# Layer 1 of the first image moves to the other instruction stream, with part of the next image's layer 0 beside it

## The chip, the core and the metric

The kernel is one program on one core of a Trainium2 chip. The time is that of the device in microseconds (us), from launch to end. A profiled execution also has a span, from the first to the last instruction. PE is TensorE, DVE is VectorE, ACT is ScalarE, POOL is GpSimd, SP is SyncE (which only issues transfers).

## What is computed

Four images of 48 channels and 256 x 256 pixels pass through four residual layers, each on a group-normalised input (16 groups of 3 channels):

```python
x = x + L0(gn(x), ...)   # 1x1 conv to 288 channels, 3x3 depthwise; q, k, v of 96 channels;
                         # product of the spectra of q and k in 8x8 patches; layer norm; times v; 1x1 conv to 48
x = x + L1(gn(x), ...)   # 1x1 conv to 288; spectrum of each 8x8 patch times a mask; 3x3 depthwise;
                         # gelu(first half) * second half; 1x1 conv to 48
x = x + L2(gn(x), ...)   # running sums of the image; two 3x3 convs give a box per pixel; the sums at the
                         # box's four corners, gathered with bilinear weights, over the box's area
x = x + L3(gn(x), ...)   # 1x1 conv to 192, 3x3 depthwise, gelu gate, 1x1 conv to 48, spectrum times a mask
```

All of it is float32. The layers of one image follow each other, and each needs the statistics (mean and deviation of each group) of the whole image before it. Images don't depend on each other.

## The kernel before, in words

`run` (L1609 on) writes two streams of work, `a` and `b`, as Python generators. Stream a has the statistics of image 0, then layer 0 and layer 1 of images 0, 1, 2, 3 in turn, then layer 3 of the four images. Stream b has the preparation of layer 1's weights (`patch_weights`), of layer 3's (`taps`), the statistics of the other images, and then layer 2 of images 0, 1, 2, 3. A generator yields numbers, its planned cost in units of its own; the stream whose sum is smaller is advanced next. A layer starts only when the one before it on the same image is written, and the stream's sum is then raised to that one's. So layer 2 of image i is written between the pieces of layers 0 and 1 of image i + 1, that of image 3 between those of layer 3, and layer 1 of image 0 has nothing beside it.

The framework then orders the instructions of each engine by dependencies, with the order of writing as the priority; instructions given to `pinned` keep the order of writing among themselves on their engine. Every engine executes its own list in order. Tiles come from pools; stream a's lie on the left of SBUF and stream b's on the right.

- `bank` (L228) gives the next of PSUM's eight banks. Five belong to stream a and two to stream b; the eighth has the tag `w4` and holds layer 2's bilinear weights. When stream b is out of work (`alone`), a takes all eight in turn.
- `dma` (L237) issues stream a's transfers from SP and stream b's from POOL. Layer 1 issues most of its own from SP by name (`queue`, L745).
- `layer0`: 128 units, in software pipelining over eight steps. In a step, `convolve` (16 products of 288 columns by `convolve2`, L391, into four banks, which ACT copies to `qkv`, L483) and `inverse` come first, then a yield of 7, then `spectra`, `turn`, `project`, `gate`, and a yield of 7 again. Each two units need a strip of the image, six transfers into two tiles A and B (`columns2`, L293), in two buffers.
- `layer1` has three phases with HBM buffers between them. Phase A (L680 to L728): 16 strips of 16 blocks; each block and half is one product (L713) into a bank, which ACT or DVE copies to `hs` (L718 and L720), and a strip is stored to `hD`. It yields 3 for each two blocks. Phase B: 36 groups of 8 channels; `around` (L765) makes the rims of the patches by four small products (L771) and eight transfers `yh<-yb`; `gated` (L784), four times for each group, fills two banks by L788 and L794, then ACT makes the Gelu (L799) and DVE the product (L800). It yields 4 after each `gated` and each `around`. Phase C: 16 strips, four pieces of each; `turn` (L856 on) transposes three banks (L865), `project` (L871 on) adds two products into one (L877). It yields 5 for each piece.
- `layer2` first makes running sums (`sums`), then 33 x 4 steps of gathers by POOL (L1126, 16 of them each), the weighing on DVE and the two convolutions of later pieces on PE.

Of the kernel before, what the change touches and what calls it, by code (L numbers as in the profile page):

```python
# [8 lines left out]
F32 = mybir.dt.float32  # L9
# [183 lines left out]
class Net:  # L193
    def __init__(self, ctx, tc, a, out):
        self.tc, self.nc, self.a, self.out = tc, tc.nc, a, out
        self.nimage = a["x"].shape[0] // C

        self.banks = {
            f: ctx.enter_context(tc.tile_pool(name="ps" + f, bufs=n, space=PSUM)) for f, n in (("a", 5), ("b", 2))
        }  # L200
        self.stream, self.alone, self.turns = "a", False, 0
        self.const = ctx.enter_context(tc.tile_pool(name="const", bufs=1))
        self.dram = ctx.enter_context(tc.tile_pool(name="dram", bufs=1, space=DRAM))
        self.stat = ctx.enter_context(tc.tile_pool(name="stat", bufs=2))
        self.n, self.fused = 0, {}
        nc, a = self.nc, self.a
        self.ident = self.load("c_ident", [128, 128])
        dft = self.load("c_dft", [128, 5, 128])
        self.fq, self.fk, self.back, self.rf, self.ri = (dft[:, i, :] for i in range(5))
        self.sel = self.load("c_sel2", [48, 506])  # L210
        self.tapsel = self.load("c_tapsel2", [128, 4, 74])
        group = self.load("c_group", [112, 208])
        self.group = {CP: group[:CP, 112:208], 112: group[:, 0:112]}
# [13 lines left out]

    def bank(self):  # L228
        if self.alone:
            self.turns += 1  # L230
            if self.turns % 8 == 0:
                return self.banks["b"].tile([128, 512], F32, name=self.nm("ps"), tag="w4", bufs=1)
            if self.turns % 8 > 5:
                return self.banks["b"].tile([128, 512], F32, name=self.nm("ps"), tag="ps")
        return self.banks[self.stream].tile([128, 512], F32, name=self.nm("ps"), tag="ps")

    def dma(self, out, of):  # L237
        (self.nc.sync if self.stream == "a" else self.nc.gpsimd).dma_start(out, of)  # L238

    def pinned(self, instruction):  # L240

        return self.tc.keep_in_program_order(instruction)

    def pool(self, name, bufs):
# [146 lines left out]
    def convolve2(self, AB, W, n, j, to):  # L391

        nc = self.nc
        A, B = AB
        half = B.shape[1]

        def full(q, b):
            for g in range(3):
                nc.tensor.matmul(  # L399
                    to(q, b), A[:, j + half * q, 128 * b + g : 128 * b + g + 128], W[:, g, :],  # L400
                    start=b == 0 and g == 0, stop=b == 1 and g == 2,
                )

        def tails(b):
            for q in range(2):
                p = slice(64 * q, 64 * q + 58)
                nc.tensor.matmul(
                    to(q, b), B[p, j, 128 * b : 128 * b + 128], W[p, 3, :], start=b == 1, stop=b == 0
                )
# [32 lines left out]
    def layer0(self, x, mr, y, xb):  # L442
        nc, a = self.nc, self.a
        st = self.stat.tile([112, 129, 6], F32, name=self.nm("st"), tag="st" + self.stream, bufs=1)
        with ExitStack() as ctx:
# [39 lines left out]
            def spectra(t):  # L485
                t.t = []
                for f, c in ((self.fq, 0), (self.fk, 96)):
                    banks = [self.bank() for _ in range(2)]
                    for h in range(2):
                        p = slice(64 * h, 64 * h + 64)  # L490
                        nc.tensor.matmul(v3(banks[h]), f[p], t.qkv[p, :, c : c + 96], start=True, stop=True)  # L491
                    for h in range(2):
# [6 lines left out]
            def inverse(t):  # L499
# [5 lines left out]
                for h in range(2):  # L505
                    nc.tensor.matmul(po[64 * h : 64 * h + 64, 0:384], self.back[:, 0:64], t.t[h][:], start=True, stop=True)
                nc.scalar.copy(  # L507
# [33 lines left out]
            def turn(t):  # L541
                pt = self.bank()
                for b in range(4):
                    nc.tensor.transpose(pt[:96, 128 * b : 128 * b + 128], t.un[:, b, :], self.ident[:])
                t.u = sb.tile([96, 512], F32, name="u", tag=f"u{t.i}{t.j}", bufs=1)
                nc.scalar.copy(t.u[:], pt[:96, :])

            def project(t, other):
# [5 lines left out]
                for i, of in ((0, other), (1, t)):  # L554
                    n = 48 if i else 64
                    nc.tensor.matmul(pp[64 * i : 64 * i + n, :], pr[:, 0:n], of.u[:], start=True, stop=True)
                for q in range(2):
# [118 lines left out]
    def layer1(self, x, mr, y):  # L676
# [4 lines left out]
        with ExitStack() as ctx:  # L681
# [25 lines left out]
            for s in range(NS):  # L707
                xt = xts[s % 3]
                hs = sb.tile([128, 8 * NG, 2, 16], F32, name="hs", tag="hs")
                for b in range(16):  # L710
                    for h in range(2):
                        ps = self.bank()
                        nc.tensor.matmul(  # L713
                            ps[:, :288], xt[64 * h : 64 * h + 49, 128 * b : 128 * b + 128],
                            win[64 * h : 64 * h + 49], start=True, stop=True,
                        )
                        if h and b % 2:
                            nc.vector.tensor_copy(hs[:, :, h, b], ps[:, :288])  # L718
                        else:
                            nc.scalar.copy(hs[:, :, h, b], ps[:, :288])  # L720
                    if b == 7 and s + 2 < NS:
                        load(s + 2)
                    if b % 2:
                        yield 3
                of = hs[:].rearrange("p (g c) h b -> p g (c h b)", c=8)
# [3 lines left out]
        with ExitStack() as ctx:  # L729
# [35 lines left out]
            def around(t):  # L765

                for e in range(4):
                    ps = self.bank()
                    for i in range(2):
                        c = 4 * i + e  # L770
                        nc.tensor.matmul(  # L771
                            ps[64 * i : 64 * i + 64, :].rearrange("p (s n) -> p s n", n=32),
                            t.wr[:, 64 * c : 64 * c + 64], t.hg[:, :, c, :], start=True, stop=True,
                        )
                    if e % 2:
# [8 lines left out]
            def gated(t, e):  # L784
                both = [self.bank() for _ in range(2)]
                for i in range(2):
                    c = 4 * i + e
                    nc.tensor.matmul(  # L788
                        both[i][:].rearrange("p (s n) -> p s n", n=32), t.wd[:, 128 * c : 128 * c + 128],
                        t.hg[:, :, c, :], start=True, stop=False,  # L790
                    )
                for i in range(2):
                    p = slice(64 * i, 64 * i + 64)
                    nc.tensor.matmul(  # L794
                        order(both[i][:]), t.wd[p, 1024 + 128 * e : 1152 + 128 * e], pick(t.yh, e)[p],
                        start=False, stop=True,
                    )
                gl = sb.tile([128, 512], F32, name="gl", tag="gl")
# [15 lines left out]
            for g in range(NG):  # L814
                t = groups[g]
                for e in range(4):
                    gated(t, e)
                    yield 4
                    if e == 0 and g + 1 < NG:
                        around(groups[g + 1])  # L820
                        if g + 2 < NG:
                            rims(g + 2)
                        yield 4
                queue(gD[:, :, g, :], t.hg[:, :, 0:4, :].rearrange("p s c n -> p s (c n)"))
# [5 lines left out]
        with ExitStack() as ctx:  # L830
# [25 lines left out]
            def turn(s, j):  # L856
                gs, got = strips[s], []
                for q in range(3):
                    pt = self.bank()
                    for b in range(4):  # L860
                        if q < 2:
                            of = gs[:, 0:96, q, 4 * j + b]
                        else:
                            of = gs[:, 96:144, :, 4 * j + b].rearrange("p c h -> p (c h)")
                        nc.tensor.transpose(pt[:96, 128 * b : 128 * b + 128], of, self.ident[:])  # L865
                    gc = sb.tile([96, 512], F32, name="gc", tag=f"gc{q}")
# [4 lines left out]
            def project(s, j, got):  # L871
                xt, yt = buffers[s % 2]
                pp = self.bank()
                for last in range(2):
                    for h in range(2):
                        n = 48 if h else 64
                        nc.tensor.matmul(  # L877
                            pp[64 * h : 64 * h + n, :], pr[:, h if last else 2, 0:n], got[2 if last else h][:],
                            start=not last, stop=bool(last),
                        )  # L880
                whole = lambda t: t.rearrange("p (b r c) -> p b r c", b=4, r=8)
# [17 lines left out]
            for s in range(NS):  # L899
                for j in range(4):  # L900
# [6 lines left out]
                    if j == 3 and s + 2 < NS:  # L907
                        gated(s + 2)
                    yield 5
            project(*last)  # L910
# [698 lines left out]
    def run(self, layers=(0, 1, 2, 3)):  # L1609
# [4 lines left out]

        a = [("first", 0)] + [(n, i) for i in images for n in (0, 1) if n in layers] + [(3, i) for i in images if 3 in layers]
        b = ([("weights", 0)] if 1 in layers else []) + ([("taps", 0)] if 3 in layers else [])
        b += [("first", i) for i in images[1:]]
        b += [(2, i) for i in images if 2 in layers]
# [8 lines left out]
        def advance(f):  # L1627
            self.stream = f
            self.alone = not todo["b"]
            if now[f] is None:  # L1630
                n, i = todo[f][0]
                if n not in ("first", "weights", "taps"):
# [3 lines left out]
                    at[f] = max([at[f]] + [done[k] for k in need])  # L1636
                now[f] = self.first_statistics(i) if n == "first" else self.patch_weights() if n == "weights" else self.taps() if n == "taps" else self.layer(n, i)
            try:
                at[f] += next(now[f])
            except StopIteration:  # L1640
# [72 lines left out]
```

## Time and profile before

| | |
|---|---|
| median of 14 runs | 18,127.32 us (18,107.94 to 18,156.39) |
| the profiled execution | 18,110.35 us |
| its span | 18,108.4 us |
| mean granted PE clock | 0.927 |
| PE, weight loads, DVE, ACT, POOL busy | 90%, 54%, 63%, 34%, 50% |
| HBM | 2,377 MB read, 832 MB written |

Where the stages lie in that span, by the first and last matmul of their lines:

| stage | us from the span's start |
|---|---|
| layer 0 of image 0 (L399), with the preparations at first | 182 to 1,832 |
| layer 1 of image 0: A (L713), B (L788), C (L865) | 1,876 to 2,126; 2,167 to 2,798; 2,817 to 3,029 |
| layer 0 of image 1, beside layer 2 of image 0 | 3,082 to 4,951 |
| layer 1 of image 1, beside the same | 5,017 to 6,589 |
| the same of image 2, beside layer 2 of image 1 | 6,638 to 10,135 |
| the same of image 3, beside layer 2 of image 2 | 10,188 to 13,685 |
| layer 3 (L1439), beside layer 2 of image 3 until 17,235 | 13,745 to 18,075 |

In the lines of the profile, `L399 PE MATMUL ps<-W,A` is an instruction of line 399 that reads the tiles W and A and writes a PSUM tile. A float32 product is two instructions there. The view by stretches gives the busy time of each engine in a piece of the span, with the number of instructions, the granted clock of PE as a share of full speed, the busy share of the 16 DMA engines and the rate. The view of waits gives how long an engine stood before instructions of a line and what ended it: in total, how often, the longest.

### The profile page before, as it was taken

Reading aid. Unit: us, or ns where it says so; the run is one execution under the profiler, and the core shown is the slowest. Engines: PE = TensorE matmul, PEld = TensorE weight load, DVE = VectorE, ACT = ScalarE, POOL = GpSimd, SP = SyncE. Lnnn points to the kernel's source line nnn. Section 1 sums busy time; section 2 is a strip of 40 time slices with the busy share of each in tenths; the row PEclk is TensorE's granted clock in tenths of the full one; section 3 lists DMA queues with packets and bytes.
Section 4 is the critical chain, followed back from the end, with each engine's and each line's share of the span. In section 5 each row is a group of like instructions: output and inputs, shape, how many; then the busy total and the mean of one; then the engine's idle time right before and its main releaser. Section 6 shows DMA issues by size and latency. Waiting matters only on the chain. (4 is left out here: it accounts for less than half of the span.)

```text
span 18108.4 us, 223197 instructions
## 1 busy us (share of the span) xinstructions
PE 16376.4 (90%) x75610; PEld 9769.5 (54%) x75610; DVE 11484.8 (63%) x24628; ACT 6121.1 (34%) x12781; POOL 9007.0 (50%) x8933
## 2 busy tenths in 40 slices
PE   8999798999978889998888899988888998889899
PEld 3556424555543355555433555554336676767778
DVE  4554323577765555777656467776565788888866
ACT  2444523444441134444412344444122221212222
POOL 1200000377765534777666157776660577777700
PEclk9999899999979999999799999987988998989999
DMA  6642887555599975555999555559997888888867
GB/s 167 187 100 57 278 287 233 137 140 144 133 297 298 285 215 134 140 142 137 325 300 288 175 141 142 142 165 317 301 286 195 203 199 198 205 195 205 204 157 164
DMA packets 1770067, 3629.80 MB, mean 200 GB/s; under 512 B 505646, under 2 KB 1279883, under 8 KB 1631784
## 3 DMA queue, kind: packets, MB, share of 16 engines
q1 hardware_dynamic: 1236272, 2319.89, 44.1%
q0 software_dynamic: 448688, 1098.99, 23.2%
q10 hardware_dynamic: 83968, 196.64, 4.4%
q8 instruction: 603, 9.88, 0.2%
q14 instruction: 536, 4.39, 0.1%
HBM read 2377.26 MB, written 832.39 MB: 177 GB/s over the span
## 5 line engine op out<-in xcount | busy, mean ns | idle before, releaser
L1126 POOL DMA_INDIRECT V<-t,idx x8192 | 8575.5, 1047 | 3624.1 <-issue 2277.4
L399 PE MATMUL ps<-W,A 128*128 128x288 f32 x12288 | 3294.8, 417 | 38.0 <-ACT t L497 16.5
L399 PEld LDWEIGHTS ps<-W,A 128*128 128x128 f32 x12288 | 2281.0, 192 | 991.5 <-issue 306.8
L1138 DVE TENSOR_TENSOR V<-V,w 128x1536 f32<-128x1536 f32 x1024 | 1764.3, 1744 | 158.3 <-DMA V<-t,idx 124.5
L1146 DVE TENSOR_TENSOR V<-V 128x1536 f32<-128x1536 f32 (+3 forms) x2048 | 1817.5, 887 | 11.2
L483 ACT COPY qkv<-ps 128x288 f32<-128x288 f32 x2048 | 766.6, 399 | 2498.6 <-PE ps L399 1277.9
L238 POOL DMA_DIRECT2D X<-x x96 | 72.6, 757 | 2930.5 <-DMA x<-yt 2008.6
L1020 PE MATMUL ps<-A,W 128*96 128x512 f32 x3072 | 1476.6, 618 | 0.0
L511 DVE BATCH_NORM_STATS2 bs<-o 128x6 f32<-128x96 f32 x2048 | 381.1, 246 | 1394.3 <-ACT o L507 1393.9
L800 DVE TENSOR_TENSOR hg<-gl,ps 128x512 f32<-128x512 f32 x576 | 394.2, 685 | 1322.0 <-ACT gl L799 1305.5
L788 PE MATMUL ps<-hg,wd 128*128 128x512 f32 x2304 | 1143.2, 619 | 43.7 <-DMA wd<-wD 43.7
L713 PE MATMUL ps<-win,xt 49*128 49x288 f32 x4096 | 941.1, 562 | 154.1 <-ACT hs L720 99.2
L799 ACT ACTIVATE gl<-ps 128x512 f32<-128x512 f32 x576 | 343.8, 597 | 1991.4 <-PE ps L794 1946.8
L794 PE MATMUL ps<-yh,wd 64*128 64x512 f32 x2304 | 715.8, 695 | 312.6 <-DMA yh<-yb 232.7
L1474 ACT ACTIVATE y<-y 128x384 f32<-128x384 f32 x512 | 267.7, 523 | 2111.7 <-DVE y L1473 2087.5
L720 ACT COPY hs<-ps 128x288 f32<-128x288 f32 x1536 | 825.5, 685 | 407.6 <-PE ps L713 253.8
L1439 PE MATMUL ps<-W,A 128*128 128x192 f32 x4096 | 927.9, 350 | 18.9 <-DVE y L1463 14.1
L1020 PEld LDWEIGHTS ps<-A,W 128*96 128x96 f32 x3072 | 477.3, 167 | 864.1 <-issue 852.4
L1439 PE MATMUL ps<-wh,A 128*128 128x192 f32 x4096 | 830.7, 349 | 118.1 <-DVE y L1463 61.4
L491 PE MATMUL ps<-qkv,c_dft_sb 64*128 64x384 f32 x4096 | 884.6, 514 | 0.0
L713 PEld LDWEIGHTS ps<-win,xt 49*128 49x128 f32 x4096 | 636.2, 251 | 443.6 <-ACT hs L720 226.1
L1439 PEld LDWEIGHTS ps<-wh,A 128*128 128x128 f32 x4096 | 732.1, 205 | 213.2 <-issue 134.7
(211 smaller groups left out, 25487.4 us busy)
## 6 DMA issues: line engine op xcount, KB each, us to landing
hg<-hD SPq DMA_DIRECT2D x144, 2048.0 KB
hD<-hs SPq DMA_DIRECT2D x60, 4608.0 KB
A<-P SPq DMA_DIRECT2D x256, 773.2 KB
gD<-hg SPq DMA_DIRECT2D x144, 1024.0 KB
gs<-gD SPq DMA_DIRECT2D x64, 2304.0 KB
V<-t,idx POOLq DMA_INDIRECT x8192
xt<-b SPq DMA_DIRECT2D x128, 896.0 KB
wd<-wD SPq DMA_DIRECT2D x144, 768.0 KB
```

The source lines that it names most:

```text
L399: nc.tensor.matmul(to(q, b), A[:, j + half * q, 128 * b + g : 128 * b + g + 128], W[:, g, :], start=b == 0 and g == 0, stop=b == 1 and g == 2,
L483: nc.scalar.copy(t.qkv[:, 2 * q + b, :], banks[2 * b + q][:, 0:288])
L491: nc.tensor.matmul(v3(banks[h]), f[p], t.qkv[p, :, c : c + 96], start=True, stop=True)
L713: nc.tensor.matmul(ps[:, :288], xt[64 * h : 64 * h + 49, 128 * b : 128 * b + 128], win[64 * h : 64 * h + 49], start=True, stop=True,)
L720: nc.scalar.copy(hs[:, :, h, b], ps[:, :288])
L788: nc.tensor.matmul(both[i][:].rearrange("p (s n) -> p s n", n=32), t.wd[:, 128 * c : 128 * c + 128], t.hg[:, :, c, :], start=True, stop=False,
L794: nc.tensor.matmul(order(both[i][:]), t.wd[p, 1024 + 128 * e : 1152 + 128 * e], pick(t.yh, e)[p], start=False, stop=True,)
L1020: m = nc.tensor.matmul(to[q], W[:, g, :], A[:, 2 * q : 2 * q + 2, g : g + 256], start=q == 0 and g == 0, stop=q == 1 and g == 2,)
L1126: nc.gpsimd.indirect_dma_start(out=V[:, k, 4 * cr : 4 * cr + 4, :].rearrange("p e c -> p (e c)"), out_offset=None, in_=table, in_offset=ba ...
L1138: self.pinned(nc.vector.tensor_mul(Vm, Vm, wm.unsqueeze(2).to_broadcast([128, 32, 48])))
L1146: self.pinned(nc.vector.tensor_add(V[:, :, 0:n, :], V[:, :, 0:n, :], V[:, :, n : 2 * n, :]))
L1439: pin(nc.tensor.matmul(of(j, b), A[:, j, k, 128 * b : 128 * b + 128], four[j], start=start, stop=stop))
```

## The change

Layer 1 of image 0 (called `early`) leaves stream a and comes to stream b, between the statistics and layer 2 of image 0. Stream a goes on from layer 0 of image 0 to layer 0 of image 1. While `early` is being written, `crossed` is set, and then:

- the yields of layer 1 are multiplied by 0.18, 0.35 and 0.05 in its three phases (`light`), so that stream b is advanced more often;
- the matmuls and transposes of layers 0 and 1 that go through `pe` keep the order of writing on PE, both streams together;
- `dma` swaps its queues: stream b's transfers go to SP, stream a's to POOL;
- stream b's third bank is the one with the tag `w4`, every third time;
- in phase A DVE copies every second bank, where it was one in four.

Outside that stage, the yields of layer 2 are multiplied by 0.96 (`pace`).

```diff
+        if self.crossed and self.stream == "b":
+            self.turns += 1
+            if self.turns % 3 == 0:
+                return self.banks["b"].tile([128, 512], F32, name=self.nm("ps"), tag="w4", bufs=1)
         if self.alone:
...
     def dma(self, out, of):
-        (self.nc.sync if self.stream == "a" else self.nc.gpsimd).dma_start(out, of)
+        (self.nc.sync if (self.stream == "a") != self.crossed else self.nc.gpsimd).dma_start(out, of)
...
+    def light(self, n, share):
+        return n * share if self.crossed else n
+
+    def pe(self, instruction):
+        return self.pinned(instruction) if self.crossed else instruction
...
-                        if h and b % 2:
+                        if h and (b % 2 or self.crossed):
                             nc.vector.tensor_copy(hs[:, :, h, b], ps[:, :288])
                         else:
                             nc.scalar.copy(hs[:, :, h, b], ps[:, :288])
...
-                        yield 3
+                        yield self.light(3, 0.18)
...
                     gated(t, e)
-                    yield 4
+                    yield self.light(4, 0.35)
                     if e == 0 and g + 1 < NG:
                         around(groups[g + 1])
                         if g + 2 < NG:
                             rims(g + 2)
-                        yield 4
+                        yield self.light(4, 0.35)
...
-                    yield 5
+                    yield self.light(5, 0.05)
...
-        a = [("first", 0)] + [(n, i) for i in images for n in (0, 1) if n in layers] + [(3, i) for i in images if 3 in layers]
+        early = (1, 0) if 1 in layers and len(images) > 1 else None
+        a = [("first", 0)] + [(n, i) for i in images for n in (0, 1) if n in layers and (n, i) != early]
+        a += [(3, i) for i in images if 3 in layers]
+        pace = {(2, i): 0.96 for i in images}
         b = ([("weights", 0)] if 1 in layers else []) + ([("taps", 0)] if 3 in layers else [])
-        b += [("first", i) for i in images[1:]]
+        b += [("first", i) for i in images[1:]] + ([early] if early else [])
         b += [(2, i) for i in images if 2 in layers]
...
+            self.crossed = todo["b"][:1] == [early] and now["b"] is not None
             try:
-                at[f] += next(now[f])
+                at[f] += next(now[f]) * pace.get(todo[f][0], 1)
```

The products at L399, L407, L491, L506, L544, L556 of layer 0 and at L713, L771, L788, L794, L865, L877 of layer 1 are wrapped in `self.pe(...)` in the same way.

More of the change, by code (lines that the diff above doesn't have):

```diff
@@ L200, in __init__ @@
         }
-        self.stream, self.alone, self.turns = "a", False, 0
+        self.stream, self.crossed, self.alone, self.turns = "a", False, False, 0
         self.const = ctx.enter_context(tc.tile_pool(name="const", bufs=1))
@@ L398, in full @@
             for g in range(3):
-                nc.tensor.matmul(
+                self.pe(nc.tensor.matmul(
                     to(q, b), A[:, j + half * q, 128 * b + g : 128 * b + g + 128], W[:, g, :],
                     start=b == 0 and g == 0, stop=b == 1 and g == 2,
-                )
+                ))
         def tails(b):
@@ L406, in tails @@
                 p = slice(64 * q, 64 * q + 58)
-                nc.tensor.matmul(
+                self.pe(nc.tensor.matmul(
                     to(q, b), B[p, j, 128 * b : 128 * b + 128], W[p, 3, :], start=b == 1, stop=b == 0
-                )
+                ))
         for q in range(2):
@@ L490, in spectra @@
                         p = slice(64 * h, 64 * h + 64)
-                        nc.tensor.matmul(v3(banks[h]), f[p], t.qkv[p, :, c : c + 96], start=True, stop=True)
+                        self.pe(nc.tensor.matmul(v3(banks[h]), f[p], t.qkv[p, :, c : c + 96], start=True, stop=True))
                     for h in range(2):
@@ L505, in inverse @@
                 for h in range(2):
-                    nc.tensor.matmul(po[64 * h : 64 * h + 64, 0:384], self.back[:, 0:64], t.t[h][:], start=True, stop=True)
+                    self.pe(nc.tensor.matmul(po[64 * h : 64 * h + 64, 0:384], self.back[:, 0:64], t.t[h][:], start=True, stop=True))
                 nc.scalar.copy(
@@ L543, in turn @@
                 for b in range(4):
-                    nc.tensor.transpose(pt[:96, 128 * b : 128 * b + 128], t.un[:, b, :], self.ident[:])
+                    self.pe(nc.tensor.transpose(pt[:96, 128 * b : 128 * b + 128], t.un[:, b, :], self.ident[:]))
                 t.u = sb.tile([96, 512], F32, name="u", tag=f"u{t.i}{t.j}", bufs=1)
@@ L555, in project @@
                     n = 48 if i else 64
-                    nc.tensor.matmul(pp[64 * i : 64 * i + n, :], pr[:, 0:n], of.u[:], start=True, stop=True)
+                    self.pe(nc.tensor.matmul(pp[64 * i : 64 * i + n, :], pr[:, 0:n], of.u[:], start=True, stop=True))
                 for q in range(2):
@@ L712, in layer1 @@
                         ps = self.bank()
-                        nc.tensor.matmul(
+                        self.pe(nc.tensor.matmul(
                             ps[:, :288], xt[64 * h : 64 * h + 49, 128 * b : 128 * b + 128],
                             win[64 * h : 64 * h + 49], start=True, stop=True,
-                        )
-                        if h and b % 2:
+                        ))
+                        if h and (b % 2 or self.crossed):
                             nc.vector.tensor_copy(hs[:, :, h, b], ps[:, :288])
@@ L770, in around @@
                         c = 4 * i + e
-                        nc.tensor.matmul(
+                        self.pe(nc.tensor.matmul(
                             ps[64 * i : 64 * i + 64, :].rearrange("p (s n) -> p s n", n=32),
                             t.wr[:, 64 * c : 64 * c + 64], t.hg[:, :, c, :], start=True, stop=True,
-                        )
+                        ))
                     if e % 2:
@@ L787, in gated @@
                     c = 4 * i + e
-                    nc.tensor.matmul(
+                    self.pe(nc.tensor.matmul(
                         both[i][:].rearrange("p (s n) -> p s n", n=32), t.wd[:, 128 * c : 128 * c + 128],
                         t.hg[:, :, c, :], start=True, stop=False,
-                    )
+                    ))
                 for i in range(2):
                     p = slice(64 * i, 64 * i + 64)
-                    nc.tensor.matmul(
+                    self.pe(nc.tensor.matmul(
                         order(both[i][:]), t.wd[p, 1024 + 128 * e : 1152 + 128 * e], pick(t.yh, e)[p],
                         start=False, stop=True,
-                    )
+                    ))
                 gl = sb.tile([128, 512], F32, name="gl", tag="gl")
@@ L864, in turn @@
                             of = gs[:, 96:144, :, 4 * j + b].rearrange("p c h -> p (c h)")
-                        nc.tensor.transpose(pt[:96, 128 * b : 128 * b + 128], of, self.ident[:])
+                        self.pe(nc.tensor.transpose(pt[:96, 128 * b : 128 * b + 128], of, self.ident[:]))
                     gc = sb.tile([96, 512], F32, name="gc", tag=f"gc{q}")
@@ L876, in project @@
                         n = 48 if h else 64
-                        nc.tensor.matmul(
+                        self.pe(nc.tensor.matmul(
                             pp[64 * h : 64 * h + n, :], pr[:, h if last else 2, 0:n], got[2 if last else h][:],
                             start=not last, stop=bool(last),
-                        )
+                        ))
                 whole = lambda t: t.rearrange("p (b r c) -> p b r c", b=4, r=8)
```

## The prediction

> **What bounds the kernel now.** The page comes first: TensorE (PE) is busy for 90% of the span and no other engine is near, so the places to look for are those where PE idles.
>
> ```profile
> span 18108.4 us, 223197 instructions
> PE 16376.4 (90%) x75610; PEld 9769.5 (54%) x75610; DVE 11484.8 (63%) x24628; ACT 6121.1 (34%) x12781; POOL 9007.0 (50%) x8933
> PE   8999798999978889998888899988888998889899
> POOL 1200000377765534777666157776660577777700
> ```
>
> POOL gathers for layer 2 and stands still in slices 5 to 7: that is layer 1 of image 0, the one layer 1 that has no layer 2 beside it. The view by stretches then prices each stage (columns: stretch and length, busy time of PE, its weight loads, DVE, ACT, POOL, granted PE clock, DMA share, GB/s):
>
> ```profile
> 1832.00:2145.00 313.00, 229.71 (x1099) 153.97 (x1098) 108.13 (x196) 213.48 (x417) 0.00 (x0) 0.76 0.88 295
> 2145.00:2800.00 655.00, 585.29 (x1728) 187.38 (x1728) 152.10 (x218) 130.69 (x217) 0.00 (x0) 0.96 0.85 280
> 2800.00:3030.00 230.00, 213.10 (x1270) 117.33 (x1272) 82.87 (x189) 99.78 (x193) 0.00 (x0) 0.96 0.84 285
> 6970.00:8505.00 1535.00, 1508.96 (x6724) 868.25 (x6723) 1162.46 (x2795) 680.57 (x1503) 1156.58 (x1106) 0.99 0.52 138
> 8505.00:8945.00 440.00, 360.42 (x1428) 223.09 (x1426) 283.21 (x523) 239.00 (x438) 315.47 (x315) 0.73 0.92 292
> 8945.00:9835.00 890.00, 758.54 (x2320) 266.39 (x2320) 487.23 (x795) 151.31 (x248) 523.28 (x543) 0.91 0.93 291
> 9835.00:10140.00 305.00, 243.74 (x1348) 132.57 (x1348) 192.55 (x343) 103.60 (x196) 151.79 (x149) 0.88 0.85 269
> ```
>
> The first three rows are phases A, B and C of layer 1 of image 0, alone: 1,198 us with 170 us of PE idle, DMA at 0.84 to 0.88. The fourth is layer 0 with layer 2: PE 98% busy, bound by PE. The last three are layer 1 of another image with layer 2: DMA at 0.85 to 0.93, PE at 80 to 85%. So PE work leaves a PE-bound stage and goes into one with PE idle and DMA nearly full. What ends PE's waits there (the waits of PE in phases A, B and C):
>
> ```profile
> PE ps L713 <- ACT hs L720: 38.1, 14, 5.8
> PE ps L771 <- DMA wr<-wD: 28.7, 11, 24.7
> PE ps L794 <- DMA yh<-yb: 27.7, 15, 4.0
> PE ps L794 <- DMA wr<-wD: 21.1, 13, 2.7
> PE ps L865 <- DMA gs<-gD: 17.8, 1, 17.8
> ```
>
> **How much is filled in.** In the planner's own units layer 0 is 128 steps of 14, with its tail 1,799. Layer 1 in the other stream now counts 128 x 3 x 0.18 = 69 in phase A, 5 + 179 x 1.4 = 256 in B, 64 x 0.25 = 16 in C: 341. So 341/14 = 24.4 of image 1's 128 layer 0 units run inside this layer 1; that is 19%.
>
> **Term 1, the work taken out of the PE-bound stage.** A layer 0 unit has 24 matmul instructions at L399. Between 1,200 and 1,800 us layer 0 ran alone and issued 1,356 of them: 56.5 units in 600 us, 10.62 us each, at PE 100% busy. 24.4 x 10.62 = **-259 us**. Beside layer 2 a unit takes 1535/109 = 14.08 us; the 3.46 us more are layer 2's, and stay.
>
> **Term 2, the growth of the layer 1 stage.** Phase A, 250 us from first to last L713: its stream gets three PSUM banks instead of five. What a bank turn costs is seen in the patch weights at the start, which ran on the other stream's two banks (the timeline; in brackets PE's idle time before):
>
> ```profile
> 34.20 2.02 PE L623 MATMUL ps<-sh,dw 9*96 9x512 f32 x4 [0.71 <-DVE tt L627]
> 36.99 2.02 PE L623 MATMUL ps<-sh,dw 9*96 9x512 f32 x4 [0.77 <-DVE tt L627]
> ```
>
> 0.77 us from the end of a fill to the next fill of that bank. A fill in A is two instructions of 0.40 us (shortest at L713), so a bank turns in 1.57 us, three give one each 0.52 us, 512 fills take 268 us. Add 69/14 x 10.62 = 52 us of layer 0, less one hidden turn at each of 10 half steps (8): 312, **+62**. The 128 copies that go from ACT (683 ns) to DVE (651 ns) unload the engine that PE waited for, but the banks now end first; I book nothing for them. Bounds: +7 if fills keep 0.40 us per pair half (205 + 52), +73 without the hidden turns.
>
> Phase B: in the timeline a `gated` step repeats every 3.00 us and an `around` takes 3.65: 144 x 3.00 + 36 x 3.65 = 563, plus 35 of loads at its start (24.7 and 10.1) and 49 of short waits at L794 make 647 of the 655 seen. With layer 0, 256/14 x 10.62 = 194 us come in, one half step (7 units) for each group of five yields (5 x 1.4). It usually falls between `around` and its reader, so the eight small transfers get 3 or 8 us more; I leave a third of the 49: 563 + 35 + 16 + 194 = 808, **+161**. Bounds: +145 with all short waits gone; +194 with all kept; and ACT adds to it, since layer 0's ACT work (about 6 us a unit by rows of 0.40 to 0.57 us, 110 us in B) can stand before a Gelu: half of it would be 55 more.
>
> Phase C: 16/14 units, **+12** (0 if the 17.8 us wait takes it). DMA is no bound: 0.85 x 655 plus layer 0's own 0.21 (its share between 1,200 and 1,800 us) x 194 is 598 of B's 816. The chain from the statistics to the first L713, 44 us, stays: the matmuls are in order of emission and layer 0's second half step comes after it. Together **+235**.
>
> Layer 0's transfers of this piece (12.2 strips of six column loads, block loads and stores, weights) go from SP to POOL. POOL has 0.00 busy in the three rows above and issues such a transfer in 0.50 to 0.75 us, so some 90 of them cost 45 to 70 us of an idle queue: nothing. Behind a store that waits there stand only the next strip's columns, double buffered, and a strip now lasts two groups of B and more, some 90 us. Without that cover a landing late by 5 us (the longest kind in the same columns on SP: 15.3 us in 3 waits) would cost 12 x 5 = 60. [...]
>
> **Term 3, layer 2 denser.** At 0.96 a layer 2 is 3,091 units of stream a, not 3,220. Over the three images 130 layer 2 units move from beside layer 0 (3.46/14 = 0.25 us each) to beside layer 1 ((1635 - 1198)/1429 = 0.31 us each): **+8**. In the last stage 129 units' worth of layer 3 pass from beside layer 2 to the stretch alone. If times add (alone 0.76 us a unit: 858 us for 1,132), this is nothing; if layer 2 alone set the pace there, 129 x 0.76 = +98. POOL is 72% busy there and 75% beside layer 0, so I take 0.
>
> **Term 4, boundaries.** Around 3,050, 6,600 and 10,150 us both streams change layer together and PE idles 25, 26 and 28 us in 100. Now a boundary of one stream falls into the middle of a layer of the other: I take half, **-40** (0 to -80). At 17,200 to 17,350, PE idles 36 us while the last layer 3 waits for the last layer 2; that now ends 173 units earlier than its reader starts: **-25**.
>
> **Sum.** -259 + 235 + 8 - 40 - 25 = -81 on the profiled execution's 18,110.35: 18,029. The median of the 14 runs is 17 above that execution, so **18,046 us**. About 0.2% (36 us) is what a measurement of this kernel can tell from no change.
>
> **Rivals.** *PE packs*: phase A +7, B +145, C +5, boundaries -80 and -36: -259 + 157 + 8 - 116 = -210, 17,917 us. For it: PE idles 170 us here, and the granted clock of phase A is 0.76 against 1.00 in unbroken layer 0. Against: the waits at the starts of phases are ahead of the filler in the same order. [...]
>
> *Serial*: layer 0 costs its full 259 in the stage and the banks of A another 21, the boundaries pay nothing, the end 25: -259 + 280 + 8 - 25 = +4, 18,131 us, no change. The +98 of layer 3 on top of the forecast gives much the same (18,144). That so little fills in that nothing is seen is in here too.
>
> *Bank turns, slower*: with three banks every fill in B's 144 `gated` steps and every fill in `around` (144) waits one turn: 288 x 0.77 = 222, so -81 + 222 = +141, 18,268 us. The timeline of B has a Gelu of 0.60 us end 0.28 us before the matmul that would want its bank begins; one ACT copy of layer 0 (0.40 us, L483) ahead of it eats that. Against: after each half step all three banks are free. It decides from 164 of the 288 on, where the time passes 36 us above before. [...]
>
> **Chances.** The forecast 0.48 (17,950 to 18,091), PE packs 0.20, serial 0.14, bank turns 0.18. Faster 0.68, same 0.14, slower 0.18. The range, 17,900 to 18,200, leaves out about 1 in 10 above and less below.
>
> **What would show it.** Layer 1 of image 0 ends near 3,265 instead of 3,030 and L399 has some 585 instructions of image 1 before that; L713 takes about 310 us and L788 about 800; clock in the stage up from 0.90 to 0.96 or more; column loads at L238 on POOL there; no wait above 1 us for banks in B (ACT gl or DVE hg ahead of L788 or L771); idle at the boundaries under 15 us in 100; layer 3 alone at the end for some 956 us. The forecast is wrong if that first stage ends after 3,330, or if layer 1 beside layer 2 takes over 30 us longer than its 1,635.

## The result, and the profile after

The changed kernel takes 18,310.83 us (median of 6 runs, 18,292.47 to 18,329.88) where the kernel before takes 18,130.55 beside it: a ratio of 1.010, 95% interval 1.009 to 1.011. It is 180 us slower. The forecast had been 18,046, and 18,311 is above the range. The profiled execution took 18,317.53 us, its span 18,315.7. When e1 to e4 of the experiments ran, the kernel before itself took 22,541.91 us on a chip where it took some 18,118 twice later (e2's trace of that time has standstills of PE, DVE and ACT beside layer 2, the longest ahead of L399 25 us), so that of those four only the first stage, which has no layer 2, is read. The change adds ten lines ahead of layer 0 and layer 1, so L399 is now L409, L713 is L723, L788 and L794 are L798 and L804, and L1126 is L1136.

The page hardly shows it: as many matmuls, PE busy for 179 us more, a single 6 in the row of the clock, in the fifth slice.

```profile
span 18315.7 us, 223122 instructions
PE 16554.9 (90%) x75610; PEld 9828.9 (54%) x75610; DVE 11566.3 (63%) x24756; ACT 6126.2 (33%) x12685; POOL 9066.4 (50%) x9021
PE   8999999999888889998888899988888988888899
POOL 1200000067776652777766257776650677777600
PEclk9999699999979999999799999987999988989899
```

The stretches of the changed kernel, in the columns of before: phases A, B and C of layer 1 of image 0 with layer 0 beside them, then layer 0 of image 2 with layer 2, then phases A, B and C of layer 1 of image 2 with layer 2.

```profile
1877.00:2290.00 413.00, 394.50 (x1236) 226.07 (x1236) 175.46 (x295) 178.91 (x296) 8.73 (x17) 0.59 0.66 220
2290.00:3100.00 810.00, 765.28 (x2660) 302.73 (x2660) 238.84 (x493) 246.41 (x466) 29.15 (x56) 0.98 0.76 243
3100.00:3350.00 250.00, 236.88 (x1365) 129.14 (x1365) 90.11 (x200) 109.12 (x213) 0.00 (x0) 0.98 0.77 258
7166.00:8553.00 1387.00, 1337.74 (x5944) 769.52 (x5943) 1032.68 (x2468) 611.61 (x1332) 1043.84 (x997) 0.99 0.51 136
8553.00:8990.00 437.00, 367.45 (x1452) 224.96 (x1450) 294.20 (x543) 243.37 (x442) 328.87 (x324) 0.73 0.91 296
8990.00:9895.00 905.00, 763.05 (x2334) 268.57 (x2334) 505.68 (x834) 151.85 (x249) 563.11 (x576) 0.91 0.93 292
9895.00:10230.00 335.00, 269.01 (x1411) 144.05 (x1410) 223.22 (x397) 107.35 (x200) 218.10 (x214) 0.86 0.86 269
```

Phase A is the odd row: PE busy for 96% of the stretch, at a granted clock of 0.59 (0.76 before). By first and last L723 it takes 399 us where L713 took 250. B takes 773 (631 before) and C 238 (212).

Where the time went is easiest to follow along layer 2, image by image, since its four runs follow each other without a pause and end shortly before the kernel does. "Start" is the first matmul of the running sums.

| us | before | changed | difference |
|---|---|---|---|
| start of layer 2 of image 0 | 3,047.3 | 3,368.7 | +321.4 |
| from there to the start of image 1's | 3,558.9 | 3,464.8 | -94.1 |
| to that of image 2's | 3,546.5 | 3,473.5 | -73.0 |
| to that of image 3's | 3,547.9 | 3,522.2 | -25.7 |
| to the end of the last gather | 3,528.8 | 3,523.3 | -5.5 |
| to the end of the span | 879.1 | 963.2 | +84.1 |
| sum, the span | 18,108.4 | 18,315.7 | +207.3 |

Layer 2 starts 321 us later, since layer 1 of image 0 has 24 units of layer 0 in it (the 25th starts at 3,270), and it wins back only 198 us of that, although each of its runs is now planned over 4% less work of the other stream.

### The profile page after: what moved, and what is told of

The parts are those of the page before. It is cut to its first block, busy times and chain, and to the rows that moved or that the text cites. A ratio compares the mean times of both kernels' runs of the same rounds, so it can differ in the third digit from the quotient of the medians.

```text
span 18315.7 us, 223122 instructions
## 1 busy us (share of the span) xinstructions
PE 16554.9 (90%) x75610; PEld 9828.9 (54%) x75610; DVE 11566.3 (63%) x24756; ACT 6126.2 (33%) x12685; POOL 9066.4 (50%) x9021
## 5 line engine op out<-in xcount | busy, mean ns | idle before, releaser
L1136 POOL DMA_INDIRECT V<-t,idx x8192 | 8587.3, 1048 | 3518.4 <-issue 2277.9
L409 PE MATMUL ps<-W,A 128*128 128x288 f32 x12288 | 3339.4, 421 | 68.6 <-ACT t L507 30.2
L409 PEld LDWEIGHTS ps<-W,A 128*128 128x128 f32 x12288 | 2298.4, 194 | 1037.7 <-issue 317.9
L798 PE MATMUL ps<-hg,wd 128*128 128x512 f32 x2304 | 1145.2, 619 | 42.3 <-DMA wd<-wD 34.0
L723 PE MATMUL ps<-win,xt 49*128 49x288 f32 x4096 | 1075.7, 607 | 106.2 <-ACT hs L730 71.5
L1449 PE MATMUL ps<-W,A 128*128 128x192 f32 x4096 | 931.2, 351 | 30.2 <-DVE y L1473 14.3
L804 PE MATMUL ps<-yh,wd 64*128 64x512 f32 x2304 | 713.6, 694 | 268.7 <-DMA yh<-yb 192.3
L723 PEld LDWEIGHTS ps<-win,xt 49*128 49x128 f32 x4096 | 677.7, 266 | 483.3 <-ACT hs L730 230.2
L1449 PE MATMUL ps<-wh,A 128*128 128x192 f32 x4096 | 829.8, 348 | 108.2 <-DVE y L1473 54.0
L1449 PEld LDWEIGHTS ps<-wh,A 128*128 128x128 f32 x4096 | 734.0, 205 | 204.0 <-issue 127.3
L1042 ACT ACTIVATE hm<-ps,b 96x512 f32<-96x512 f32 x512 | 349.4, 683 | 1446.3 <-PE ps L1039 855.3
```

The lines of the kernel that those rows point to most:

```text
L409: self.pe(nc.tensor.matmul(to(q, b), A[:, j + half * q, 128 * b + g : 128 * b + g + 128], W[:, g, :], start=b == 0 and g == 0, stop=b == 1 ...
L723: self.pe(nc.tensor.matmul(ps[:, :288], xt[64 * h : 64 * h + 49, 128 * b : 128 * b + 128], win[64 * h : 64 * h + 49], start=True, stop=True,))
L798: self.pe(nc.tensor.matmul(both[i][:].rearrange("p (s n) -> p s n", n=32), t.wd[:, 128 * c : 128 * c + 128], t.hg[:, :, c, :], start=True, ...
L804: self.pe(nc.tensor.matmul(order(both[i][:]), t.wd[p, 1024 + 128 * e : 1152 + 128 * e], pick(t.yh, e)[p], start=False, stop=True,))
L1136: nc.gpsimd.indirect_dma_start(out=V[:, k, 4 * cr : 4 * cr + 4, :].rearrange("p e c -> p (e c)"), out_offset=None, in_=table, in_offset=ba ...
L1449: pin(nc.tensor.matmul(of(j, b), A[:, j, k, 128 * b : 128 * b + 128], four[j], start=start, stop=stop))
```

## The experiments

Two theories stood after the result. For the first stage, theory K: phase A has only three banks, which makes PE fill and wait in turn, and PE's granted clock then falls (0.59 in A); its rival F: layer 0's bursts in one order with it slow it down. For the rest, theory P: the denser planning (0.96) costs time beside layers 0 and 3; its rival O: the offset between the streams does. Theory G came later and took P's place.

Of e1 to e4 the first stage is read; e5 and e7 are the kernels of e1 and e2 once more, without the standstills.

### e3 and e4: phase A alone, with three banks and with five

```diff
-                        yield self.light(3, 0.18)
+                        yield self.light(3, 0)          # e3 and e4: nothing of layer 0 in phase A
...
+        if self.crossed and self.stream == "b" and self.wide:   # e4: wide in phase A
+            return self.banks["a"].tile([128, 512], F32, name=self.nm("ps"), tag="ps")
```

e3: 

> The changed kernel with nothing of layer 0 in phase A of layer 1 (its share of 0.18 becomes 0); three banks, order and queues stay. Theory K (three banks make the matmuls of A wait for copies one by one, and PE then runs at half its clock, 0.59 granted, so a fill takes 0.74 us instead of 0.52): phase A takes about 380 us, against 400 with the fill, the clock of A stays near 0.5 to 0.6, and the total is within 40 us of the changed kernel. Rival F (layer 0's bursts in the same order are what slow A): A falls to about 270 us at a clock of 0.75 or more and the total by 60 to 80 us.

e4: 

> As e3 (nothing of layer 0 in phase A), and phase A takes its banks from the five of the other stream, which stands still then. Theory K: A falls to about 250 us as before the change, clock 0.75 or more, and the total to about 18,311 - 150 + 52 = 18,215. If the queues or the order on PE were the cause instead, A stays above 350 us.

By first and last matmul phase A took 361 us in e3 and 252 us in e4. (The whole of e3 took 22,539.97 us, 1.0010 of the kernel before beside it with an interval of 0.9992 to 1.0027, that of e4 22,399.47 us, 0.9947 with 0.9926 to 0.9969.) These are the rows of A in the view by stretches, e3 first:

```profile
1877.00:2238.00 361.00, 358.71 (x1064) 215.37 (x1062) 165.59 (x260) 166.15 (x260) 1.42 (x3) 0.52 0.69 235
```

```profile
1877.00:2129.00 252.00, 198.74 (x1072) 146.89 (x1072) 151.94 (x268) 149.73 (x260) 2.01 (x4) 0.82 0.98 336
```

With three banks PE is "busy" for 99% of the stretch at a clock of 0.52; with five it is busy for 79% at 0.82 and ends 109 us earlier, now with DMA at 0.98. So the banks lengthen A, not layer 0's bursts: with them A took 399, that is 38 us more for 52 us of layer 0. The 99% counts the matmuls alone. The turns through the banks show in the weight loads ahead of them: in e3's A these stood idle for 140 us, 137 of it until a copy had emptied a bank.

```profile
L723 PEld LDWEIGHTS ps<-win,xt 49*128 49x128 f32 x1022 | 208.2, 303 | 140.0 <-ACT hs L730 68.7 <-DVE hs L728 68.7 <-DMA win<-win 1.6
```

Inside A of e3 the clock stays at one half:

```profile
1910.00:2230.00 320.00, 320.00 (x933) 193.70 (x932) 149.99 (x233) 150.32 (x233) 0.00 (x0) 0.50 0.75 258
```

The timeline of PE in the changed kernel shows how the clock comes in:

```profile
1948.37 10.97 PE L723 MATMUL ps<-win,xt 49*128 49x288 f32 x30
1959.27 4.40 PE L409 MATMUL ps<-W,A 128*128 128x288 f32 x12
1963.60 1.24 PE L417 MATMUL ps<-W,B 58*128 58x288 f32 x8
1964.77 3.18 PE L409 MATMUL ps<-W,A 128*128 128x288 f32 x12
1967.88 1.23 PE L723 MATMUL ps<-win,xt 49*128 49x288 f32 x6
1969.35 1.24 PE L723 MATMUL ps<-win,xt 49*128 49x288 f32 x6 [0.24 <-ACT hs L730]
1970.85 1.25 PE L723 MATMUL ps<-win,xt 49*128 49x288 f32 x6 [0.25 <-DVE hs L728]
```

Ahead of a burst of layer 0, 30 instructions or 15 fills take 10.97 us, 0.73 each, at a granted clock of 0.50 (1,948 to 1,959). The burst starts slow too (4.40 us for twelve that take 3.18 a little later; the clock is 0.78 from 1,960 to 1,964 and 1.00 from 1,964 to 1,967). Right after it three fills take 1.5 us, 0.50 each, at a clock of 1.00 (1,968 to 1,972): the cadence of three banks that the prediction had worked out as 0.52. That cadence holds for a few fills; from 1,972 to 2,000 the clock is 0.50 again. That the clock is lower with few banks is shown by e3 against e4 (0.52 and 0.82); why it is while PE counts as busy is not.

### e9: without the order of writing on PE

```diff
     def pe(self, instruction):
-        return self.pinned(instruction) if self.crossed else instruction
+        return instruction
```

> The changed kernel without the order of writing on PE in the crossed stage (`pe` returns the instruction as it is). If that order is what makes the first stage long, it ends 60 us or more before 3,346; theory K (banks and clock) has phase A at 360 us or more all the same, and the stage's end within 40 us of 3,346.

The one run took 18,335.34 us. A is 403 us from first to last L723, at a clock of 0.60, and C ends at 3,394 instead of 3,346. The order of writing is not what makes the stage long. Without it the stage ends 48 us later (theory K had allowed 40), with 720 of L409's instructions in it instead of 612: 4.5 units of layer 0 more, which at 10.62 us are 48.

### e7: the denser planning alone

```diff
-                at[f] += next(now[f])
+                at[f] += next(now[f]) * (0.96 if todo[f][0][0] == 2 else 1)
```

e2, with the standstills: 

> The kernel before with one edit, layer 2's yields times 0.96; streams, banks and queues as before. Theory P: slower by 90 to 160 us (18,220 to 18,290), most of it in the last stage. Rival O: within 40 us of before, since the streams still start each layer 2 together with a layer 0.

e7, the same kernel: 

> The same kernel as e2 (before, layer 2's yields times 0.96), on a chip without the standstills. Theory P: 18,220 to 18,290. Rival O: within 40 us of before.

e2 gave 22,556.59 us, a ratio of 1.0012 (0.9994 to 1.0029), which decides nothing. e7 gave 18,281.70 against 18,140.49: 1.0075 (1.0058 to 1.0091), 141 us slower, as theory P had it. So 0.96 by itself loses time with everything else as before. In e7's trace some 20 us of it lie in each of layer 2's first three periods and 97 behind the last gather. The reason is in the counts of POOL in equal stretches beside layer 0: before, then e7, then the changed kernel.

```profile
7250.00:8450.00 1200.00, 1177.03 (x5258) 678.31 (x5257) 931.19 (x2199) 531.34 (x1175) 936.80 (x893) 0.99 0.54 142
```

```profile
7300.00:8500.00 1200.00, 1164.57 (x5083) 669.92 (x5083) 911.16 (x2160) 517.82 (x1137) 936.22 (x891) 0.97 0.55 142
```

```profile
7300.00:8500.00 1200.00, 1154.11 (x5125) 665.42 (x5125) 917.74 (x2169) 526.75 (x1149) 936.10 (x890) 0.98 0.52 139
```

POOL issues 893, 891 and 890 instructions in 1,200 us, whatever the planning. It is PE's count that falls, from 5,258 to 5,083 and 5,125. And the waits of POOL in that stretch of before say that it never waits for anybody for more than 0.3 us:

```profile
POOL V L1126 <- issue: 255.0, 837, 0.3
```

937 us busy and 837 pauses of 0.3 us, one ahead of nearly every gather, make 1,192 of the 1,200. The page counts 78% of the stretch as busy; POOL is occupied for 99%. A gather costs 1.07 + 0.30 = 1.37 us. That is theory G: beside layer 0 POOL is full. Beside layer 3 it is nearly so, before and in e7:

```profile
14200.00:17000.00 2800.00, 2474.10 (x14575) 1958.29 (x14573) 2321.80 (x4209) 581.96 (x1176) 2046.12 (x1907) 0.91 0.86 200
```

```profile
14300.00:17100.00 2800.00, 2436.45 (x14121) 1921.86 (x14120) 2279.90 (x4146) 566.58 (x1143) 2036.42 (x1907) 0.90 0.86 197
```

Of the 2,800 us of before POOL is busy for 2,046, pauses for 474 under "issue" and waits 201 for transfers of earlier gathers. So layer 2 can hardly be made to pass faster there; planning it denser thins out the other stream.

### e5 and e6: layer 2 at pace 1 in the changed kernel

```diff
-        pace = {(2, i): 0.96 for i in images}
+        pace = {}
```

e1, with the standstills: 

> The changed kernel with layer 2's yields counted in full again (pace 1 instead of 0.96); all else of the change stays. Theory P (the denser layer 2 is what lost time after the first stage: the last gather came 3,537 us after the last stage's start where it was 3,543, so layer 2 set the pace there and 129 units of layer 3 went to the end alone, about 98 us, and 50 to 70 us more beside layers 0 and 1): 18,311 falls to about 18,150 to 18,190, the last layer 3 alone takes about 880 us after the last gather instead of 965. Rival O (the offset between the streams, not the density): stays at 18,280 to 18,340.

e5, the same kernel: 

> The same kernel as e1, since the chip of the first four runs needed 22,542 us for the kernel before and stood still beside every layer 2, which hides what the pace does. On a chip where before takes about 18,130: theory P (density) 0.7 to 0.9% under the changed kernel, that is 18,150 to 18,190; rival O (offset of the streams) 18,280 to 18,340.

e6 (with e4's edits): 

> e4 and e1 together: no fill in phase A, its five banks back, layer 2 at pace 1. The first stage ends at 3,189 as in e4 (that stage has no layer 2 and was not disturbed): 157 us earlier than in the changed kernel for 52 us less of layer 0. Theory P: 18,311 - 105 - 140 = 18,066, 60 us under before. Rival O: 18,311 - 105 = 18,206.

e1 gave 22,495.55 us, 0.9985 (0.9970 to 1.0000), again undecided. e5 gave 18,285.55: 1.0076 (1.0059 to 1.0093). That is rival O's number, and theory P's 18,150 to 18,190 was missed; but it is not O's mechanism. By its last L875, layer 1 of image 3 ends at 13,639 us, 46 ahead of before: the offset as such costs nothing on the way. From the end of the first stage to there stream a needs 365 us less than before: about Term 1's 259 and 341 units of layer 2, at the prediction's 0.25 to 0.31 us each, that now come later. But layer 2, from its first matmul to its last gather, takes 14,127 us where it took 14,182. So the offset is still there at the end, and the last layer 3 waits for the last layer 2. This is e5 between the third and the fourth layer 3:

```profile
17290.00:17540.00 250.00, 41.43 (x173) 28.87 (x172) 133.69 (x194) 4.50 (x8) 163.89 (x159) 0.55 0.39 99
```

PE works 41 of 250 us. e6 gave 18,216.39, 1.0039 (1.0025 to 1.0053), again P's number missed (18,066) and O's (18,206) met, with a wait of the same kind (PE works 37 of 195 us). So pace 0.96 buys this wait off, by losing about as much elsewhere.

### h1, h2, h3: POOL relieved

These three kernels leave out the gathers of two of a box's four corners and read twice the length at the other two. Their output is not that of the layer; they tell of time alone.

```diff
                 for k in range(4):
-                    for cr in range(4):
+                    for cr in range(2):
                         nc.gpsimd.indirect_dma_start(
-                            out=V[:, k, 4 * cr : 4 * cr + 4, :].rearrange("p e c -> p (e c)"),
+                            out=V[:, k, 8 * cr : 8 * cr + 8, :].rearrange("p e c -> p (e c)"),
```

h1, on the kernel before: 

> The kernel before with two gathers of double length for each pixel column instead of four (the two lower corners are left out; as many bytes, half as many instructions on POOL). Theory G: POOL is the bound beside layers 0 and 3, because each gather occupies it for 1.04 us and 0.30 us that the page does not count as busy (893 gathers in 1,200 us before, 891 in e7, 890 in the changed kernel, whatever the pace): 200 to 500 us under before, most of it beside layer 3. Rival P (the density itself, by order and collisions on PE): within 100 us of before.

h2, on the changed kernel: 

> The changed kernel with the same edit as h1. Theory G: with POOL free, a later start of layer 2 can be made up, and only the first stage's own loss is left (316 us longer for 259 us of layer 0), less the boundaries: 0 to +70 us against h1. Rival P: +150 to +200 us against h1, as without the edit.

h3, on e4: 

> e4 (no fill in phase A, its five banks back, pace 0.96) with the two long gathers of h1 and h2: both causes taken away at once. If the two causes are all there is, the first stage ends near 3,189 with 206 us of layer 0 in it for 159 us of growth, that is 104 us better than in h2, and the rest goes as in h2: 0.9971 of before less 0.0057, a ratio near 0.991, and under h1's 0.9953. If the banks' loss was made up further on anyway, or a third cause is left, it stays at h2's ratio or above h1's.

| | us | ratio to before, measured beside it | 95% interval |
|---|---|---|---|
| h1, before | 18,045.29 | 0.9953 | 0.9936 to 0.9970 |
| h2, changed | 18,077.70 | 0.9971 | 0.9961 to 0.9981 |
| h3, changed, five banks in A and no fill there | 17,968.10 | 0.9913 | 0.9899 to 0.9926 |

The change cost 180 us on the kernel as it is; with POOL relieved it costs 32 (18,077.70 - 18,045.29, the two intervals overlap). In the profiled executions, layer 2's three periods shrink by 123, 124 and 72 us from h1 to h2, and the stretch from the last start to the last gather by 78, where the changed kernel had 94, 73, 26 and 5 against before. That is theory G's test, and it holds. (The third period shrinks less in both. By the planner's units, two periods of 129 have then used up 258 of the offset's 341; in h3 with its 272 only 14 are left, and its third period is 17 us under h1's.) h3 adds the five banks, and the sign turns: it is 77 us under h1, and its interval lies wholly below. Its ratio is the 0.991 that the two causes together had been expected to give.

The size of h1's own gain was missed: 73 us against 200 to 500. In 1,200 us beside layer 0 POOL now has 466 instructions and waits, but PE is at 1,180 us, where it had 1,177: there the kernel before has POOL and PE full at once, and freeing one alone brings little.

```profile
7250.00:8450.00 1200.00, 1180.38 (x5259) 678.43 (x5257) 935.50 (x2216) 535.40 (x1182) 462.74 (x466) 0.99 0.52 142
```

The waits of POOL in h1 show the change of roles:

```profile
POOL V L1126 <- DVE res L1148: 503.3, 42, 20.1
POOL V L1126 <- issue: 113.0, 371, 0.3
```

### e8: five banks, and a pace that uses up the offset

```diff
-        pace = {(2, i): 0.96 for i in images}
+        pace = {(2, i): 0.972 for i in images[:-1]}    # and e4's edits
```

> e4 (no fill in phase A, five banks there) with pace 0.972 for the first three layers 2, which takes up the 272 units of the offset, and 1 for the last one. Theory G: layer 2's chain starts at 3,189 instead of 3,030, and its periods beside layer 0 cannot shrink; it gets back 20 to 40 us a period at most from the stretch beside layer 1: 18,150 to 18,230, slower than before. If the work simply added up it would be 18,080.

18,155.17 us, 1.0019 (1.0010 to 1.0029): the lower end of theory G's numbers, 75 us above those of work that simply adds up, and still 37 us over before. No variant with all its gathers that ran without the standstills beat the kernel before. e4, with pace 0.96, ran only with them (0.9947); whether it gains without them is not known.

## Why the prediction was wrong

In the profiled execution the span grew by 207 us where the sum had -81. The 288 between them come in three parts. The first stage grew by 316 instead of 235 (Term 2). From its end to the last L875 of layer 1 the changed kernel won back 188, where Terms 1, 3 and 4 have -291. From there to the end it lost 79, where -25 was forecast. With POOL relieved the last two are -314 and +1 (the profiled executions of h2 and h1, of which h2's is 7 us shorter, while the medians have it 32 longer), so these two misses are one: POOL was taken as an engine with time to spare.

**How much is filled in: right.** 341 planned units, 24.4 of layer 0. L409 starts its 25th unit at 3,270 us, and 612 of its instructions lie before the end of the stage, where some 585 were expected. That end, 3,346, is past the 3,330 that the prediction had named as its sign of being wrong.

**Term 1, -259: the step that failed.** The time of PE per unit (10.62 us) stands, but it was taken as a gain because the stage it left was "bound by PE". It was bound by PE and POOL together, and POOL's part was misread: the prediction took POOL as "72% busy there and 75% beside layer 0" from the busy column, while 0.30 us ahead of each gather stood under "issue" in the waits. PE time taken out of a stretch in which POOL is 99% occupied shortens it only as far as gathers leave it too, and the gathers moved on to stretches that were full as well. With POOL relieved the 259 appear.

**Term 2, +235, was +316.** Phase B was near: +142 by its first and last matmul, +161 forecast. PE's waits there are 7.7 us for banks and 6.8 at L804, where L794 had 49 before:

```profile
PE ps L798 <- ACT gl L809: 7.7, 8, 1.0
PE ps L804 <- DMA wr<-wD: 3.6, 4, 1.5
PE ps L804 <- DMA yh<-yb: 3.2, 2, 2.1
```

Phase C grew by 26 instead of 12. Phase A grew by 149 instead of 62, and its upper bound (which should read +70, from 268 + 52 - 250) lies far under that as well. Three banks at 0.50 us a fill were right at a clock of 1.00 (1,968 to 1,972); the missing 87 is the clock, 0.59 over the whole of A, which the sum had left at one. The rows of e3 (0.52 with three banks) and e4 (0.82 with five) agree in that fewer banks go with a lower clock, here for float32 matmuls on 49 rows, and e3's clock stays at 0.50 for 320 us. The prediction had looked only for a clock that rises when PE is filled, from 0.90 to 0.96 or more in the stage; here PE was filled, by its busy time (96% in A), and the clock fell: from 0.76 to 0.59 in A, from 0.90 to 0.87 in the stage (1,840 to 3,346).

**Queues: right.** Layer 0's columns came from POOL without one wait of PE for them in the stage; in the rows above POOL is busy for 9 of 413 us in A and 29 of 810 in B.

**Term 3, +8 and 0 for layer 3.** The other value named there, +98 "if layer 2 alone set the pace there", was the right one: the last stage, from the last L875 on, took 4,502 us instead of 4,423 (+79), and the last gather ended 3,523 us after layer 2's last start, where it was 3,529. With POOL relieved the last stage is as long as before (4,420 against 4,419). Beside the denser layer 2, layer 1 of image 2 takes 1,677 us in the rows above, 42 more than its 1,635: the prediction's other sign of being wrong.

**Term 4, -40 and -25: not found.** PE idles 28 us between 6,600 and 6,700 and 36 between 10,150 and 10,250, where stream a changes layer: as much as at the joint boundaries (26 and 28). Layer 2's own boundaries, now in the middle of a layer 0, cost next to nothing (1 us between 6,780 and 6,880). So the idle time belongs to stream a and stayed whole, where half had been taken off. The pause of L1449 between the third and fourth layer 3 is 49 us (17,503 to 17,553) against 53.

```profile
6600.00:6700.00 100.00, 71.73 (x350) 44.95 (x350) 69.22 (x143) 24.24 (x55) 77.55 (x76) 0.85 0.62 167
6780.00:6880.00 100.00, 98.92 (x520) 65.03 (x516) 54.95 (x162) 49.16 (x126) 11.24 (x16) 1.00 0.39 112
```

**The rivals.** "Bank turns" had the sign, but not the cause: in B, where it looked, PE waited 7.7 us for banks, and in A it was the clock that went down with them. (By its own numbers it would have decided from 152 turns on, not 164.) "PE packs" came true by the busy row of A, 96%, and was slow all the same. None of the rivals had layer 2's chain, which starts when layer 1 of image 0 ends: whatever is filled in ahead of it delays it.

## What to carry to other kernels

Before work is moved out of a stage because one engine is full there, look for a second one that is full too, by counts in equal stretches before and after and not by the busy column: POOL's 0.30 us of "issue" before each gather were occupied time, not idle time. Ask which chain the filled-in work delays; here a stage's idle time was filled at nearly the price of a later start for the four runs of layer 2 behind it. And a matmul stream that has to turn through few PSUM banks may lose its clock too, as in phase A here (0.52 with three banks in e3, 0.82 with five in e4), so price it at half clock as well.

## What the runs showed of the hardware that was not expected

- A row with PE 99% busy had a granted clock of 0.52 (e3, phase A), and one with PE 79% busy 0.82 (e4): here the busy share did not tell the clock.
- A gather of twice the bytes costs POOL the same: 1,024 ns in h1 beside layer 0, against 1,066 for the single ones in the same stretch of before.
- In e2's trace PE, ACT and DVE stood still together again and again beside layer 2, at times while POOL went on with its gathers: in 1,200 us L399 waited 60.6 us in 26 pauses, the longest of 25 us, for nothing that the profile shows. What did it stays open.
